# Reordering the probability transposes, one set of statistics and the tails of a two-layer graph kernel

## The chip, the cores and the metric

The kernel runs on one core of one Trainium2 chip, in one launch. The metric is the device time in microseconds of that core. The kernel before was run three times: 2000.07, 2002.58 and 2004.22 us, median 2002.58. A further execution was taken by the hardware profiler; the trace and every profile line here come from that one.

## The reference

The input x is 128 graphs of 128 nodes with 512 features, `adj` is a 128 by 128 matrix. All arithmetic is in float32.

```python
# layer 0: W1 = W2 = adj, so C - A is the bias alone
A = einsum('od,bdn->bon', adj, x)
out = max(relu(A[:, :, None, :] + b), axis=-1)     # one number per graph and row
x = layernorm(x + out)
# layer 1: attention with 8 heads of 64, masked by adj == 0
q, k, v = split(x @ w_qkv)
attn = softmax(where(adj == 0, -inf, q @ k.T / 8))
o = (attn @ v) @ w_proj + b_proj
o = o + layernorm(o) * ln_gamma + ln_beta
x = layernorm(x + o)
```

So each graph goes through one layer norm after layer 0 ("y"), one on the projected attention ("o") and one on the final sum ("z").

## The kernel before, in words

A tile is one graph, 128 nodes on the partitions by 512 features. Four tiles make a group (g, 32 of them), two tiles a pair (q). The three large products (QK, V and the output projection) are done a group at a time by Winograd's form of Strassen's method: a `Unit` has seven half-size products instead of eight. `product(i)` issues the eight matmuls of product i into one of four PSUM banks (b1 to b4; bank 1 takes 1, 6 and 7, bank 2 takes 2, bank 3 takes 5 and 3, bank 4 takes 4). `snap(k)` is a ScalarE copy of bank 1 after products 1, 6 and 7 (k = 1, 2, 3). `result(half, col)` is a VectorE addition of a bank and a snap: (0, 0) reads bank 2 and snap 1, (0, 1) bank 3 and snap 2, (1, 0) bank 4 and snap 3, (1, 1) bank 3 and snap 3. Product 3 adds into bank 3 only after result(1, 1) has read it, and product 6 into bank 1 only after snap 1. Products 5, 6, 7 and 3 need sums of input quarters (`x_sums`, `o_sums`, made mostly on GpSimd by `run_sums`); 1, 2 and 4 take the quarters as they are. The weights have such sums too (`weight_sums`, GpSimd).

The order of the work is written out by hand: `pin` keeps each instruction in program order on its engine, and each engine runs its own list in order. DMAs go through the queue of SP, which is in order too.

The main loop (p = 0 to 60) handles one pair, tiles a = 2p and b = 2p+1, beside one unit of QK for the next group (`first`) and one unit of V or of the output projection (`second`; V where p is odd, but for p = 0, whose first unit is V and whose second is QK). For each tile: `scores` (TensorE), `softmax_max` (VectorE), `softmax_exp` (ScalarE, eight heads), `softmax_div` (VectorE), then the probabilities must be transposed across partitions. `prob_transpose` makes 32 by 32 block transposes into the tile `pu` (VectorE, L421), `prob_write` sends it to a buffer `hop` in DRAM (one DMA, L430), and `prob_read` fetches it back in the other order as `pT` (four DMAs, L441). `prob_move` is the three in a row. `attend` (TensorE, PSUM tile `po`) multiplies pT with V in the next iteration; `attend_copy` takes it out (ScalarE).

Meanwhile later pairs pass through layer 0 (`l0_mm`, `l0_max`, `l0_add`, `l0_norm`, and the same way through DRAM: `l0_transpose`, `l0_write`, `l0_read`, the latter x1T), and earlier ones through their tails: `one` or `stats` takes the mean and variance of tiles (`bn`, two VectorE instructions of 0.66 and 0.18 us each), `finish_stats` makes scale and shift of them (GpSimd, three small instructions), `tail_inner` and `tail_outer` apply them (ScalarE), `tail_residual` does the three additions and multiplications (GpSimd), `tail_store` or `tail_outer_one` writes the output. `tail_fused` does the inner norm and the residual of one tile in three VectorE instructions.

Before the loop, the head runs layer 0 for the first ten tiles and QK of group 0 in two units, with the statistics "first", "second" and "third". After the loop, the tail (from `before, o_u, v_u = ...`) does the last three output projections, of which the last half group (tiles L-3 to L, L = 127) goes through `last_project`, a plain product with the whole weight.

Of the kernel before, what the change touches and what calls it, by code (L numbers as in the profile page):

```python
# [9 lines left out]
F32 = mybir.dt.float32  # L10
# [6 lines left out]
def kernel(  # L17
# [31 lines left out]
    B, P, D = x.shape  # L49
# [3 lines left out]
    G = 4  # L53
    GT = G * P
    HT = GT // 2
    HE = D // 2
# [58 lines left out]
    def weight_sums(w, cols, width):  # L115
        t = w[:, :, :, ds(cols, width)]
        b11, b21, b22, b12 = (t[:, i] for i in range(4))
        tt(nc.gpsimd, t[:, 4], b12, b11, ALU.subtract)
        tt(nc.gpsimd, t[:, 6], b22, b12, ALU.subtract)
        tt(nc.gpsimd, t[:, 5], b22, t[:, 4], ALU.subtract)  # L120
        tt(nc.gpsimd, t[:, 3], b21, t[:, 5], ALU.subtract)
# [273 lines left out]
    def softmax_exp(b, heads=range(H)):  # L395
        if 0 in heads:
            psums[b] = small.tile([P, H], F32, tag="sums", name=f"sums_{b}")
        for i in heads:
            pin(
                nc.scalar.activation(  # L400
                    prob[b][:, i],
                    prob[b][:, i],
                    AF.Exp,
                    bias=nmax[b][:, i : i + 1],
                    accum_out=psums[b][:, i : i + 1],
                )
            )
# [195 lines left out]
    def stats(name, *items):  # L603

        mv = small.tile([P, NC, 2], F32, tag="mv", name=f"mv_{name}")
        for k, (kind, b) in enumerate(items):
            bn({"o": o_of, "z": zs.get, "y": xs.get}[kind](b), mv, k)
        finish_stats(mv, items)
        return mv
# [32 lines left out]
    for q in range(2):  # L642
        l0_beta(q)
        l0_spill(q)
    cur.result(0, 0)
    cur.product(6)
    cur.snap(2)
    cur.product(5)
# [2 lines left out]
    for f in range(G, 2 * G):  # L651
        l0_max(f)
        l0_add(f)
    cur.product(4)
    cur.product(7)
    stats("second", *(("y", f) for f in range(G, 2 * G)))
    before = cur


# [2 lines left out]
    weight_load(wp, w_proj, 0, HE, 0, HE)  # L662
    ga_bc = broadcast(nc.sync, "ga_bc", ln_gamma)
    bp_bc = broadcast(nc.sync, "bp_bc", b_proj)
    weight_sums(wv, 0, HE)
    before.snap(3)
    before.result(1, 1)
    before.result(1, 0)
    for f in range(G, G + 2):
        l0_norm(f)  # L670
    cur.product(2)
# [34 lines left out]
    for p in range(LAST + 1):  # L706
# [66 lines left out]
        if p == 0:  # L773
            first.snap(2)
            scores(a)
            scores(b, ("po", "pa"))
            softmax_max(a)
            softmax_max(b)
            softmax_exp(a)
            softmax_exp(b)  # L780
        else:
            softmax_exp(b, range(4))
            first.snap(2)
            softmax_exp(b, range(4, H))
        first.product(5)
        first.product(4)
        first.product(7)
        if n is not None:
            l0_read(n)
        softmax_div(a)  # L790
        prob_move(a)
        if ph == 1 and tb is not None:
            one("z", zs, tb)
        if ph == 0 and ta is not None:
            one("o", o_rows, ta)
        first.snap(3)
        softmax_div(b)
        prob_move(b)
        first.result(1, 1)
        first.result(1, 0)  # L800
        if f is not None:
            for j in range(2):
                l0_mm(2 * f + j, f"pss{j}")
# [134 lines left out]
    prob_read(L - 3)  # L938
    scores(L - 1)
    v_u.result(1, 1)  # L940
    for t in range(L - 11, L - 7):
        tail_inner_one(t)
    tail_residual_one(L - 11)
    softmax_max(L - 1)
    scores(L, po_pa)
    v_u.result(1, 0)
    run_sums(o_sums(NG - 2))
    o_u = o_unit(NG - 2)
    o_u.product(1)
    o_u.snap(1)  # L950
# [5 lines left out]
    o_u.result(0, 0)  # L956
    v_u.product(3)
    v_u.result(0, 1)
    for t in range(L - 10, L - 7):
        tail_residual_one(t)  # L960
    o_u.product(6)
    softmax_exp(L, range(4))
# [4 lines left out]
    o_u.product(7)  # L967
    softmax_div(L - 1)
    prob_move(L - 1)
    attend(L - 3)  # L970
    o_u.snap(3)
    attend_copy(L - 3)
# [1 line left out]
    attend_copy(L - 2)  # L974
    tail_outer(B // 2 - 7)
    tail_store(B // 2 - 7)
    o_u.result(1, 1)
    softmax_div(L)
    prob_move(L)
    o_u.result(1, 0)  # L980
    o_u.product(3)
    o_u.result(0, 1)
    stats("last_2", ("o", L - 5), ("o", L - 4), ("z", L - 11), ("z", L - 10))
    last_project(L - 3, wlast, "b2")
    last_project(L - 2, wlast, "pss0")
    for t in (L - 5, L - 4):
        tail_inner_one(t)
        tail_residual_one(t)
    attend(L - 1)
    attend_copy(L - 1)  # L990
    for t in (L - 11, L - 10):
        tail_outer_one(t)
    last_project(L - 1, wlast, "pss1")
    stats("last_3", ("z", L - 9), ("z", L - 8), ("o", L - 7), ("o", L - 6))
    mv = stats("last_4", ("o", L - 3), ("o", L - 2))
    for t in (L - 7, L - 6):
        tail_inner_one(t)
        tail_residual_one(t)
    attend(L, "pa")
    attend_copy(L)  # L1000
    last_project(L, wlast, "b1")
    for t in (L - 9, L - 8):
        tail_outer_one(t)
    tail_fused(L - 3, mv[:, 0, 0:1])
    tail_fused(L - 2, mv[:, 1, 0:1])
    mv = stats("last_5", ("o", L - 1), ("z", L - 5), ("z", L - 4))
    mv2 = stats("last_6", ("o", L), ("z", L - 3), ("z", L - 2))
    tail_fused(L - 1, mv[:, 0, 0:1])
    for t in (L - 5, L - 4):
        tail_outer_one(t)  # L1010
    tail_fused(L, mv2[:, 0, 0:1])
    for t in (L - 3, L - 2):
        tail_outer_one(t)
    stats("last_7", ("z", L - 1), ("z", L - 7), ("z", L - 6))
    stats("last_8", ("z", L))
    for t in (L - 1, L - 7, L - 6, L):
        tail_outer_one(t)


# [39 lines left out]
```

## Time and profile before

| what | value |
|---|---|
| median of three runs | 2002.58 us |
| profiled execution, its own time | 2008.6 us |
| its span, first to last instruction | 2006.8 us |
| mean granted TensorE clock | 0.993 |
| busy: TensorE matmul, VectorE, ScalarE, GpSimd | 1956.4, 1607.1, 1055.5, 1266.7 us |
| TensorE busy from 0 to 50, 50 to 100 us | 37.94, 48.59 us |
| TensorE busy from 100 to 1900 us, in the trace's six stretches | 98.62, 396.71, 397.92, 396.99, 397.87, 98.24 us |
| TensorE busy from 1970 to 2007 us | 15.27 us |
| last matmul begins | 1988.07 us |
| issue to landing, median: hop write, pT read, x1T read | 3.7, 3.0, 3.4 us |

The page gives for each engine its busy time, its share of the span and its instructions. PE is TensorE's matmuls, PEld its weight loads, DVE VectorE, ACT ScalarE, POOL GpSimd, SP the engine that issues most DMAs. A line of a timeline reads: start in us, duration in us, engine, source line, operation, output and input by the program's names, shapes, count, and in brackets how long the engine stood idle before it and what ended that. A line of the waits reads: who waited for whom, total us, times, longest. Many operations pass through helpers, so L74 is every matmul and L77 every two-operand addition of VectorE and GpSimd; the names of the tiles tell them apart. A DMA instruction's duration is only its issue.

### The profile page before, as it was taken

To read this page: it belongs to the slowest core of one execution; us is meant where nothing else is said; L and a number is where in the kernel's file an instruction comes from. 1 tells how busy PE (TensorE), PEld (TensorE's weight loads), DVE (VectorE), ACT (ScalarE), POOL (GpSimd) and SP (SyncE) were. 2 spreads that over 40 slices of the span, in tenths; PEclk is the share of its full clock that TensorE was granted. 3 is DMA by queue.
4 is the path that set the end of the run, shared out by engine and by line. 5 is a ranking of instruction groups with operands and counts; after the bars stand their busy time and mean duration, and the time that the engine had idled before them with its cause. 6 is when DMAs were issued, how large, how long until landed. Compare 5 with 4: busy or idle time off the path is not lost.

```text
span 2006.8 us, 33038 instructions
## 1 busy us (share of the span) xinstructions
PE 1956.4 (97%) x11545; PEld 1637.6 (82%) x11545; DVE 1607.1 (80%) x2519; ACT 1055.5 (53%) x3066; POOL 1266.7 (63%) x811
## 2 busy tenths in 40 slices
PE   7999999999999999999999999999999999999995
PEld 5888888888888888888888888888888888888872
DVE  6768778778788788788787888788787887787686
ACT  3444555545545546556555555555455455455453
POOL 5336656767557676557676567576566675576646
PEclk8999999999999999999999999999999999999998
DMA  6655565565565566666556656655665655655553
GB/s 199 153 149 147 162 194 156 172 188 149 178 186 161 179 171 175 179 167 179 179 160 175 191 158 176 191 158 168 184 164 172 188 164 172 186 165 163 157 183 111
DMA packets 445655, 341.76 MB, mean 170 GB/s; under 512 B 276912, under 2 KB 378416, under 8 KB 445488
## 3 DMA queue, kind: packets, MB, share of 16 engines
q1 hardware_dynamic: 445056, 338.85, 58.7%
q8 instruction: 92, 1.51, 0.3%
q10 hardware_dynamic: 432, 0.79, 0.1%
q14 instruction: 75, 0.61, 0.1%
HBM read 172.82 MB, written 166.72 MB: 169 GB/s over the span
## 4 chain that ended last, share of the span: by engine, by line
PE 72%; DVE 13%; DMA 10%; SPq 2%; issue 2%; POOL 1%; ACT 1%; ACTq 0%; POOLq 0%; DVEq 0%
PE b_qk L74 30%; PE b_v L74 14%; PE b_o L74 13%; PE pss L74 6%; PE po L74 5%; DMA hop<-pu 5%; DVE s L77 4%; PE pa L74 3%; DMA pT<-hop 3%; DVE pu L421 2%; SPq L441 1%; DVE xt L287 1%; DVE qk L179 1%; DVE st_mv L235 1%; DVE amax L267 1%
## 5 line engine op out<-in xcount | busy, mean ns | idle before, releaser
L74 PE MATMUL b_qk<-s_x,wqk 128*128 128x256 f32 x2048 | 476.2, 381 | 4.9 <-DVE s_x L77 2.5
L74 PEld LDWEIGHTS b_qk<-s_x,wqk 128*128 128x128 f32 x2048 | 385.9, 190 | 67.6 <-DVE qk L179 11.4
L400 ACT ACTIVATE s<-s,nmax 128x128 f32<-128x128 f32 x1024 | 396.1, 391 | 7.7 <-DVE nmax L393 7.7
L74 PE MATMUL b_qk<-x1T,wqk 128*128 128x256 f32 x1536 | 361.0, 385 | 2.2 <-ACT u_v L173 1.4
L74 PEld LDWEIGHTS b_qk<-x1T,wqk 128*128 128x128 f32 x1536 | 287.9, 191 | 48.5 <-ACT u_v L173 2.2
L77 DVE TENSOR_TENSOR s<-s,rec 128x1024 f32<-128x1024 f32 x128 | 297.0, 2320 | 4.4
L246 POOL TENSOR_SCALAR rs_mv<-mv 128x6 f32<-128x6 f32 (+2 forms) x61 | 14.8, 242 | 418.1 <-DVE mv L236 418.1
L77 POOL TENSOR_TENSOR z<-z,ga_bc 128x1024 f32<-128x1024 f32 x58 | 164.8, 2841 | 177.7 <-ACT z L254 177.7
L173 ACT COPY u_qk<-b_qk 128x512 f32<-128x512 f32 x192 | 112.5, 586 | 250.8 <-PE b_qk L74 249.6
L74 PE MATMUL b_v<-wv,s_x 128*128 128x256 f32 x1024 | 237.0, 379 | 0.0
L74 PE MATMUL b_o<-wp,s_o 128*128 128x256 f32 x992 | 230.0, 380 | 1.8 <-POOL s_o L77 1.8
L381 DVE SCALAR_TENSOR_TENSOR s<-pss,mask 128x512 f32<-128x512 f32 x256 | 164.4, 684 | 70.1 <-PE pss L74 69.7
L74 PEld LDWEIGHTS b_v<-wv,s_x 128*128 128x128 f32 x1024 | 194.4, 190 | 26.8 <-DVE s L77 0.3
L74 PEld LDWEIGHTS b_o<-wp,s_o 128*128 128x128 f32 x992 | 188.1, 190 | 28.5 <-POOL s_o L77 2.2
L77 POOL TENSOR_TENSOR x<-x,be_bc 128x1024 f32<-128x1024 f32 x64 | 182.1, 2847 | 35.4 <-DVE rec L411 28.8
L179 DVE TENSOR_TENSOR v<-b_v,u_v 128x512 f32<-128x512 f32 x128 | 87.1, 681 | 138.2 <-PE po L74 133.0
L400 ACT ACTIVATION_READ_ACCUMULATOR s<-s,nmax 128x1 f32 x1024 | 194.2, 190 | 0.0
L179 DVE TENSOR_TENSOR qk<-b_qk,u_qk 128x512 f32<-128x512 f32 x256 | 167.6, 674 | 31.6 <-PE b_qk L74 16.1
L74 PE MATMUL b_v<-wv,x1T 128*128 128x256 f32 x768 | 176.2, 379 | 0.0
L173 ACT COPY u_v<-b_v 128x512 f32<-128x512 f32 x96 | 56.2, 586 | 226.4 <-PE b_v L74 226.4
L74 PEld LDWEIGHTS b_v<-wv,x1T 128*128 128x128 f32 x768 | 145.9, 190 | 32.2 <-issue 13.9
L173 ACT COPY u_o<-b_o 128x512 f32<-128x512 f32 x93 | 54.5, 586 | 222.9 <-PE b_o L74 222.8
(107 smaller groups left out, 3377.4 us busy)
## 6 DMA issues: line engine op xcount, KB each, us to landing
hop<-pu SPq DMA_DIRECT2D x128, 512.0 KB, 3.7
pT<-hop SPq DMA_DIRECT2D x512, 128.0 KB, 3.0
spill<-x SPq DMA_DIRECT2D x64, 512.0 KB, 4.3
x<-in_x_dram SPq DMA_DIRECT2D x62, 512.0 KB, 4.5
xhop<-xt SPq DMA_DIRECT2D x248, 128.0 KB, 2.3
x1T<-xhop SPq DMA_DIRECT2D x248, 128.0 KB, 3.4
xr<-spill SPq DMA_DIRECT2D x59, 512.0 KB, 3.6
out_dram<-xr SPq DMA_DIRECT2D x58, 512.0 KB, 3.6
```

The lines of the kernel that those rows point to most:

```text
L74: pin(nc.tensor.matmul(*args, **kwargs))
L77: pin(eng.tensor_tensor(dst, a, b, op))
L173: pin(nc.scalar.copy(t, self.banks[1]))
L179: nc.vector.tensor_tensor(self.out[half, col], self.banks[bank], self.snaps[k], ALU.add)
L235: pin(nc.vector.bn_stats(st, src))
L246: pin(nc.gpsimd.tensor_scalar(rs[:, :n], mv[:, :n, 1], EPS, None, ALU.add))
L267: pin(nc.vector.tensor_reduce(amax, pas.pop(f), AX.X, ALU.max))
L287: nc.vector.transpose(xts[q][:, :, :, j].rearrange("p q c b -> p c q b"), xs[2 * q + j].rearrange("p (c q a) -> p c q a", c=KC, q=Q),)
L381: nc.vector.scalar_tensor_tensor(s[:, par], pss[b][par], SCALE, mask.unsqueeze(1).to_broadcast([P, NP, P]), ALU.mult, ALU.add,)
L400: nc.scalar.activation(prob[b][:, i], prob[b][:, i], AF.Exp, bias=nmax[b][:, i : i + 1], accum_out=psums[b][:, i : i + 1],)
L421: nc.vector.transpose(u.rearrange("p q h b -> p h q b"), prob.pop(b).rearrange("p h (q a) -> p h q a", q=Q),)
L441: nc.sync.dma_start(out=pT[b][ds(q * QS, QS)].rearrange("a i h b -> a i (h b)"), in_=hop[:, :, q].rearrange("i a f -> a i f"),)
```

## The change

The change moves instructions; it adds and removes only small ones (two groups of tail statistics are merged with others).

- Head: product(4) of the first unit goes ahead of product(6); the four-tile statistics "second" go behind result(1, 1) and result(1, 0) of that unit, which stand in the next block, and ahead of the weight sums of `wv`.
- Loop: `prob_move` is taken apart. On SP the order is now: write of a, the x1T reads (`l0_read`), write of b, reads of a, reads of b. The statistics `one(...)` between the two tiles go behind the two results. For p = 0, snap(3) goes ahead of the exponentials of b.
- Tail: the sums `o_sums(NG - 2)` go ahead of the four inner norms, the residual of L-11 goes to the other three, `prob_move(L)` goes ahead of attend(L-3), attend(L) and its copy go straight behind attend(L-1), and statistics, residuals and outer norms of the last twelve tiles are dealt out anew.

```diff
     cur.result(0, 0)
+    cur.product(4)
     cur.product(6)
     cur.snap(2)
     cur.product(5)
...
-    cur.product(4)
     cur.product(7)
-    stats("second", *(("y", f) for f in range(G, 2 * G)))
     before = cur
...
-    weight_sums(wv, 0, HE)
     before.snap(3)
     before.result(1, 1)
     before.result(1, 0)
+    stats("second", *(("y", f) for f in range(G, 2 * G)))
+    weight_sums(wv, 0, HE)
...
             softmax_exp(a)
-            softmax_exp(b)
         else:
...
         first.product(7)
+        if p == 0:
+            first.snap(3)
+            softmax_exp(b)
+        softmax_div(a)
+        prob_transpose(a)
+        prob_write(a)
         if n is not None:
             l0_read(n)
-        softmax_div(a)
-        prob_move(a)
+        if p > 0:
+            first.snap(3)
+        softmax_div(b)
+        prob_transpose(b)
+        prob_write(b)
+        prob_read(a)
+        prob_read(b)
+        first.result(1, 1)
+        first.result(1, 0)
         if ph == 1 and tb is not None:
             one("z", zs, tb)
         if ph == 0 and ta is not None:
             one("o", o_rows, ta)
-        first.snap(3)
-        softmax_div(b)
-        prob_move(b)
-        first.result(1, 1)
-        first.result(1, 0)
...
     v_u.result(1, 1)
+    run_sums(o_sums(NG - 2))
     for t in range(L - 11, L - 7):
         tail_inner_one(t)
-    tail_residual_one(L - 11)
     softmax_max(L - 1)
     scores(L, po_pa)
     v_u.result(1, 0)
-    run_sums(o_sums(NG - 2))
...
-    for t in range(L - 10, L - 7):
+    for t in range(L - 11, L - 7):
         tail_residual_one(t)
...
     prob_move(L - 1)
+    softmax_div(L)
+    prob_move(L)
     attend(L - 3)
...
     tail_store(B // 2 - 7)
+    mv = small.tile([P, NC, 2], F32, tag="mv", name="mv_last_2")
+    keys = [("z", L - 11), ("z", L - 10), ("o", L - 5), ("o", L - 4), ("o", L - 7), ("o", L - 6)]
+    bn(zs[L - 11], mv, 0)
+    bn(zs[L - 10], mv, 1)
     o_u.result(1, 1)
-    softmax_div(L)
-    prob_move(L)
     o_u.result(1, 0)
+    bn(o_of(L - 5), mv, 2)
+    bn(o_of(L - 4), mv, 3)
     o_u.product(3)
     o_u.result(0, 1)
-    stats("last_2", ("o", L - 5), ("o", L - 4), ("z", L - 11), ("z", L - 10))
     last_project(L - 3, wlast, "b2")
     last_project(L - 2, wlast, "pss0")
-    for t in (L - 5, L - 4):
-        tail_inner_one(t)
-        tail_residual_one(t)
     attend(L - 1)
     attend_copy(L - 1)
+    attend(L, "pa")
+    attend_copy(L)
+    last_project(L - 1, wlast, "pss1")
+    last_project(L, wlast, "b1")
+    bn(o_of(L - 7), mv, 4)
+    bn(o_of(L - 6), mv, 5)
+    finish_stats(mv, keys)
+    for t in (L - 5, L - 4, L - 7, L - 6):
+        tail_inner_one(t)
     for t in (L - 11, L - 10):
         tail_outer_one(t)
-    last_project(L - 1, wlast, "pss1")
-    stats("last_3", ("z", L - 9), ("z", L - 8), ("o", L - 7), ("o", L - 6))
-    mv = stats("last_4", ("o", L - 3), ("o", L - 2))
-    for t in (L - 7, L - 6):
-        tail_inner_one(t)
-        tail_residual_one(t)
-    attend(L, "pa")
-    attend_copy(L)
-    last_project(L, wlast, "b1")
+    tail_residual_one(L - 5)
+    mv = stats("last_3", ("o", L - 3), ("o", L - 2), ("z", L - 9), ("z", L - 8))
+    tail_residual_one(L - 4)
     for t in (L - 9, L - 8):
         tail_outer_one(t)
     tail_fused(L - 3, mv[:, 0, 0:1])
     tail_fused(L - 2, mv[:, 1, 0:1])
-    mv = stats("last_5", ("o", L - 1), ("z", L - 5), ("z", L - 4))
-    mv2 = stats("last_6", ("o", L), ("z", L - 3), ("z", L - 2))
+    mv = stats("last_4", ("o", L - 1), ("z", L - 3), ("z", L - 2))
+    tail_residual_one(L - 7)
     tail_fused(L - 1, mv[:, 0, 0:1])
+    for t in (L - 3, L - 2):
+        tail_outer_one(t)
+    mv = stats("last_5", ("o", L), ("z", L - 5), ("z", L - 4))
+    tail_residual_one(L - 6)
+    tail_fused(L, mv[:, 0, 0:1])
     for t in (L - 5, L - 4):
         tail_outer_one(t)
-    tail_fused(L, mv2[:, 0, 0:1])
-    for t in (L - 3, L - 2):
-        tail_outer_one(t)
-    stats("last_7", ("z", L - 1), ("z", L - 7), ("z", L - 6))
-    stats("last_8", ("z", L))
-    for t in (L - 1, L - 7, L - 6, L):
+    stats("last_6", ("z", L - 1), ("z", L - 7))
+    stats("last_7", ("z", L), ("z", L - 6))
+    for t in (L - 1, L - 7, L, L - 6):
         tail_outer_one(t)
```

## Prediction

> **What bounds the kernel now.** First the engine line and the clock line of the page: TensorE is busy 97% of the span at full clock, so time can come only from the few stretches in which it stands still, or from the ends.
>
> ```profile
> PE 1956.4 (97%) x11545; PEld 1637.6 (82%) x11545; DVE 1607.1 (80%) x2519; ACT 1055.5 (53%) x3066; POOL 1266.7 (63%) x811
> PEclk8999999999999999999999999999999999999998
> ```
>
> Second, the waits of TensorE over the span (total us, times, longest).
>
> ```profile
> PE po L74 <- DMA pT<-hop: 11.5, 19, 1.2
> ...
> PE b_qk L74 <- DVE s_x L77: 2.5, 1, 2.5
> ...
> PE b_qk L74 <- ACT u_v L173: 1.4, 1, 1.4
> ...
> PE b_qk L74 <- ACT u_qk L173: 0.7, 1, 0.7
> ```
>
> In the main loop only the transposed probabilities pT come late, and by little. The waits of the weight loads add one that the matmul rows hide:
>
> ```profile
> PEld b_qk L74 <- DVE qk L179: 11.4, 28, 2.1
> ```
>
> These are 28 times that product(3) of the first unit waits for VectorE to read bank 3 (result(1,1)). Third, TensorE's timeline at the `po` groups. Its late ones look like this, always the second group, tile b:
>
> ```profile
> 1054.54 1.09 PE L74 MATMUL po<-pT,v 128*64 128x128 f32 x16
> 1056.84 1.09 PE L74 MATMUL po<-pT,v 128*64 128x128 f32 x16 [1.21 <-DMA pT<-hop]
> ```
>
> From the start of one iteration's first po group to the next I get 60 periods. The shortest are 29.97 us for even p and 30.18 us for odd p; what all 60 have above these sums to 16.0 us, the full price of late pT. Fourth, the queue of SP in one iteration:
>
> ```profile
> 1007.66 2.75 SPq L318 DMA_DIRECT2D x1T<-xhop  x4
> 1010.46 0.82 SPq L430 DMA_DIRECT2D hop<-pu  x1
> 1014.38 1.73 SPq L441 DMA_DIRECT2D pT<-hop  x4
> 1016.21 0.38 SPq L430 DMA_DIRECT2D hop<-pu  x1
> 1019.81 1.73 SPq L441 DMA_DIRECT2D pT<-hop  x4
> ```
>
> The write of b stands behind the reads of a, which stand until the write of a has landed. Fifth, the chain of waits in the head, which ends in TensorE's 0.7 us wait:
>
> ```profile
> 39.89 0.19 DVE mv_second L236
> ...
> 40.16 0.23 POOL rs_mv_second L246
> ...
> 41.84 1.52 ACT x L254 x2
> 43.35 0.48 ACT u_qk L173
> ...
> 43.97 3.69 PE b_qk L74 x16
> ```
>
> Last, the tail: VectorE restarts at 1981.91 and sets the end; TensorE waits for a copy that ScalarE does late.
>
> ```profile
> 1981.91 0.75 DVE L595 SCALAR_TENSOR_TENSOR z<-z,rs_mv_last,pp 128x512 f32<-128x512 f32 x1 [5.86 <-POOL rs_mv_last L77]
> ...
> 1982.96 5.18 PE L74 MATMUL pp<-wlast,oT 128*128 128x512 f32 x8 [3.17 <-ACT oT L471]
> ```
>
> [...] a hop write lands a median 3.7 us after its issue, and SP issues nothing in between. [...] the division `s<-s,rec` takes 1.22 us beside an idle POOL and 2.0 to 2.75 us beside a busy one. [...] the clock records change on a grid of 3.413 us; after the window at 1979.15, with 0.63 us of matmuls, the clock is 0.5 for 3.41 us; after windows with 1.36 us it drops and with 1.68 us it does not.
>
> **The change, part by part.** All sums are against the profiled execution (2008.6 us, span 2006.8); its 6.0 us above the median of 2002.58 stay out, and I subtract the sum from the median.
>
> *Loop, pT.* Taking the iteration shown: the two statistics of 0.8 us between the tiles go behind the results, so pu of b is ready 1.6 us sooner (1015.1 to 1013.5). The write of a goes at about 1009.6 (its pu ends at 1009.5), the four x1T reads behind it at 1010 to 1012.8, the write of b at 1013.5 instead of 1016.2, the reads of a at 1013.9 (hop landed at 1013.3), those of b at 1013.5 + 3.7 = 1017.2 instead of 1019.8. That is 2.6 us sooner; in even p the same count gives 3.8. The worst period lost 1.4 us, so the margin covers nearly all; I leave 1.0 us for stray slow landings: **-15.0** (bounds -16.0 and -8). Moved with it: x1T reads 2.3 us later (used some ten us later by the next group's sums; hidden), and out, spill, reload and load issues some 2 us sooner (they wait for nothing that moves). Reads of a start within 0.5 us of before.
>
> *Loop, product(3).* Statistics now follow result(1,1), which ends near 1014.1 instead of 1015.65; product(3) is due at 1015.6. The stall is two steps of about 0.105 us (108 and 104 ns above the usual matmul spacing) in 28 odd iterations: 28 x 0.21 = **-5.9** (bounds -5.9 and 0). l0_max keeps its place, since VectorE's total ahead of it is unchanged.
>
> *Head.* product(4) needs no sums, so its 1.73 us fill the 2.5 us wait before product(6). But this frees TensorE only to wait elsewhere. The statistics "second" leave VectorE at 36.77 and now stand behind result(1,1) and (1,0), which wait for snap(3), which follows the last l0_add on ScalarE (37.65) and takes 0.6: results 38.25 to 39.5, statistics 39.5 to 43.0 instead of 36.77 to 40.27. Queued behind them: POOL's rs and sh (1.65), two norms (1.5), snap(1) (0.5); product(6) of the second unit, which needs bank 1 read, starts at 46.7 instead of 43.97: **+2.75** (bounds +1.5, +3.2). TensorE is out of work from 41.8, so one window lies nearly empty and the next runs at half clock: 3.41/2 = **+1.7** (0 to +3.4). All that follows is TensorE-bound to 68.8, so nothing gives this back. Weight sums of wv slip from 46.8 to 49.5 on POOL; used at 57.8 + 4, hidden.
>
> *p = 0.* snap(3) no longer follows the exp of b: the 1.41 us wait at 70.22 goes. But exp(b) then runs 67.65 to 70.75 instead of 66.5 to 69.6, division and transpose of b end 1.1 us later, and result(1,1) behind them at 74.1 instead of 73.05; product(3), due at 72.2, starts at 74.2 instead of 73.78: **+0.4** (bounds -1.4, +2.1 with a clock drop).
>
> *Tail.* Sums s_o ahead of the residual of L-11: the 1.75 us wait at 1949.57 goes, but product(5) still waits for v_u.result(0,1) (VectorE, to 1950.94): -0.3. Division and pu of L fill VectorE's idle 1954.4 to 1960; write of L goes behind the reads of L-1 at 1962, its pT lands near 1970, before it is used at 1972.9; the output of pair 57 stands behind these on SP, 4 us later, and nobody waits for it. attend(L) follows attend(L-1), so TensorE ends near 1983.3 instead of 1989.2, but that end was not last. The tail_inner of L-5 now stands behind attend_copy(L) on ScalarE (1974.6), one residual (3.95) and rs (1.4) follow on POOL: VectorE restarts at 1980.85 instead of 1981.91. From there: two fused tails 5.0, three statistics 2.4, rs 1.3, rest of a fused tail 1.7, statistics 2.4, rs 1.3, 1.7; POOL's last residual (4.4) ends at about 1999, two rs chains (2.5) and two norms (1.5) follow: last output issued near 2003.4 instead of 2003.75. **-0.4** (bounds -1.5, +1.5). The new statistics waits are the price: VectorE did 18.5 us without one.
>
> **Sum:** -15.0 - 5.9 + 2.75 + 1.7 + 0.4 - 0.4 = -16.45; 2002.58 - 16.45 = **1986.1** (profiled execution: about 1992).
>
> **Rivals.**
> *Half of the loop's gain.* Three hop writes and reads overlap more, landings grow past 3.7 us and b's margin shrinks: pT gives -8, or the product(3) step stays (it may be the cost of a changed operand, not of a wait; against that, even p do not have it). Time: 1986.1 + 6 or 7 = 1992.5.
> *Head hidden.* If the norms wait less than I count, or no clock drop comes (-2.9), and p = 0 and the tail fall at their good ends (-1.8 and -1.1), the time is 1980. For it: the page shows only 3.2 us of waits in the head. Against: the chain of norms is plain.
> *Slower: SP blocked by b.* Reads of a now stand behind the write of b. They land at about 1018.7 and are used at 1024.6: 5.9 us of margin. If b's pu slips by more than that (division behind a slow POOL), every further 0.1 us costs 60 x 0.1 = 6 us, and the -15 is lost too. At 0.3 us past the point: 2002.6 + 18 + 4.5 = 2025. Against: the dearest division seen costs 1.5 us extra.
> *Nothing.* Loop gives only product(3) (-5.9) and head takes 4.9: 2001.5.
>
> **Chances.** Forecast 0.58 (1983 to 1990), half gain 0.18, head hidden 0.15, nothing 0.05, slower 0.04. The range leaves out the last two and the edges: 1979 to 1996. A change under 0.2% (4 us) can't be told from none here. Faster 0.92, same 0.04, slower 0.04.
>
> **What would show it.** The row of po waits on pT falls from 11.5 us to under 1.5; periods are 29.97 for both parities; SP shows two hop writes before eight pT reads; a wait of about 5 us for u_qk near 46.7 and a half clock after it; a wait of product(3) for qk or v near 77 (shifted). A po wait in the first group would make me wrong, as would a product(6) that starts before 45.

## The result and the profile after

| kernel | runs | median, us | lowest to highest, us |
|---|---|---|---|
| before | 4 | 2002.80 | 2000.07 to 2004.22 |
| changed | 4 | 1987.91 | 1985.16 to 1988.53 |

The ratio is 0.9925 [0.9907, 0.9942]: 14.9 us less (11.6 to 18.6 by the interval). That is some 1.8 us above the 1986.1 predicted and well inside its range. The profiled execution of the changed kernel took 1988.53 us, its span 1986.7 us. It is one of the four runs, while the profiled execution of before (2008.6 us) lay 6 us above the median of its kernel.

The page first, its engine line, its clock line and the shares of the chain that ended last, by engine:

```profile
PE 1946.4 (98%) x11545; PEld 1644.8 (83%) x11545; DVE 1565.2 (79%) x2518; ACT 1055.1 (53%) x3066; POOL 1293.7 (65%) x808
PEclk8999999999999999999999999999999999999997
...
PE 95%; DVE 2%; DMA 1%; POOL 1%; ACT 0%; issue 0%; SPq 0%; ACTq 0%; POOLq 0%; DVEq 0%
```

In before the same line read:

```profile
PE 72%; DVE 13%; DMA 10%; SPq 2%; issue 2%; POOL 1%; ACT 1%; ACTq 0%; POOLq 0%; DVEq 0%
```

Now it is TensorE nearly from end to end: the chain no longer leaves it in the loop for the way of the probabilities through DRAM. The waits of TensorE say what is left (who waited for whom, total us, times, longest):

```profile
PE b_qk L74 <- ACT u_qk L173: 3.9, 1, 3.9
...
PE b_v L74 <- DVE v L179: 2.0, 1, 2.0
...
PE po L74 <- DMA pT<-hop: 1.0, 1, 1.0
```

The waits on pT fell from 11.5 us in 19 to 1.0 us in one, and that one is in the tail. The rows for s_x (2.5 us) and for u_v (1.4 us) are gone; the row for u_qk grew from 0.7 to 3.9 us (in the head), and that for v (2.0 us, at p = 0) is new; the prediction named both. In the weight loads' waits the row of 28 waits on qk, 11.4 us in all, is no longer there.

The queue of SP in one iteration (issue start, issue duration):

```profile
1001.48 0.34 SPq L430 DMA_DIRECT2D hop<-pu  x1
1001.86 3.20 SPq L318 DMA_DIRECT2D x1T<-xhop  x4
1005.11 1.11 SPq L430 DMA_DIRECT2D hop<-pu  x1
1006.31 4.76 SPq L441 DMA_DIRECT2D pT<-hop  x8
```

The write of a goes first, the four x1T reads behind it, then the write of b, and only then the eight reads of pT.

The span can be cut in three by the starts of TensorE's po groups: up to that of p = 1 (the head and p = 0), from there to that of p = 61, and the rest.

| stretch, us | before, as shown | before, profiled again | changed |
|---|---|---|---|
| start to the first po group | 82.51 | 81.74 | 87.25 |
| p = 1 to p = 61 | 1820.33 | 1813.92 | 1794.76 |
| p = 61 to the end | 103.95 | 103.92 | 104.74 |
| span | 2006.8 | 1999.6 | 1986.7 |

In the changed kernel 58 of the 60 periods are 29.97 us and the last two, which have no matmuls of layer 0, 28.25 us: 58 x 29.97 + 2 x 28.25 = 1794.8. The loop is TensorE's own work and nothing else. It gained 19.2 to 25.6 us, and the head and p = 0 gave 4.7 to 5.5 us of it back.

### The profile page after: what moved, and what is told of

Same layout as the page of the kernel before. It is cut to its first block, busy times and chain, and to the rows that moved or that the text cites. A ratio compares the mean times of both kernels' runs of the same rounds, so it can differ in the third digit from the quotient of the medians.

```text
span 1986.7 us, 33036 instructions
## 1 busy us (share of the span) xinstructions
PE 1946.4 (98%) x11545; PEld 1644.8 (83%) x11545; DVE 1565.2 (79%) x2518; ACT 1055.1 (53%) x3066; POOL 1293.7 (65%) x808
## 4 chain that ended last, share of the span: by engine, by line
PE 95%; DVE 2%; DMA 1%; POOL 1%; ACT 0%; issue 0%; SPq 0%; ACTq 0%; POOLq 0%; DVEq 0%
PE b_qk L74 39%; PE b_v L74 19%; PE b_o L74 19%; PE pss L74 6%; PE po L74 6%; PE pa L74 5%; PE pp L74 0%; POOL zl L77 0%; DMA x<-in_x_dram 0%; DMA wqk<-in_L_gnn_w_qkv_dram 0%; DVE s_x L77 0%; DMA hop<-pu 0%; DVE st_mv_last L235 0%; DVE z L77 0%; POOL rs_mv_last L77 0%
## 5 line engine op out<-in xcount | busy, mean ns | idle before, releaser
L74 PEld LDWEIGHTS b_qk<-s_x,wqk 128*128 128x128 f32 x2048 | 391.8, 191 | 58.1 <-POOL wv L77 4.3
L77 DVE TENSOR_TENSOR s<-s,rec 128x1024 f32<-128x1024 f32 x128 | 252.3, 1971 | 4.4
```

Source lines behind the costliest of these rows:

```text
L74: pin(nc.tensor.matmul(*args, **kwargs))
L77: pin(eng.tensor_tensor(dst, a, b, op))
```

## The experiments

My theory: in the loop two separate causes go, the late pT of tile b and the stall of product(3) behind the statistics; in the head the delayed norms and a clock drop give some 5 us back; p = 0 and the tail are worth under 1 us. The rivals are those of the prediction: a loop gain of half the size, a head that costs nothing, and SP's new order as a danger. Medians of the kernels are compared with one another directly, though the batches of experiments ran on three different chips. The median of before itself was 2002.80 us beside the changed kernel and 2004.37, 2001.14 and 1999.38 us in the batches. Its late pT differ from execution to execution, as shown below; what part the chip has in this was not separated. The kernels without late pT repeat within 0.6 to 4.0 us, and `old_p0` and `old_tail`, which should lie within 0.6 us of the changed kernel, came within 0.7 us of it in another batch.

### The loop alone, and its two halves

`loop_only` is before with the change of the loop and nothing else: the head, the tail and the two exponentials and snap(3) of p = 0 are as before. Against before:

```diff
+        softmax_div(a)
+        prob_transpose(a)
+        prob_write(a)
         if n is not None:
             l0_read(n)
-        softmax_div(a)
-        prob_move(a)
-        if ph == 1 and tb is not None:
-            one("z", zs, tb)
-        if ph == 0 and ta is not None:
-            one("o", o_rows, ta)
         first.snap(3)
         softmax_div(b)
-        prob_move(b)
+        prob_transpose(b)
+        prob_write(b)
+        prob_read(a)
+        prob_read(b)
         first.result(1, 1)
         first.result(1, 0)
+        if ph == 1 and tb is not None:
+            one("z", zs, tb)
+        if ph == 0 and ta is not None:
+            one("o", o_rows, ta)
```

> The kernel before with the loop's part of the change alone (head, first iteration and tail as before). My theory: the loop gives all of the gain and head, first iteration and tail cost some 5 us of it (in the profiled executions the first po group starts 4.7 us later and the stretch from the last iteration to the end is 0.7 us longer), so this is FASTER than the full change: about 1982.5 us, every period 29.97 us. Rival, the later start of the full change is only the jitter of the first loads: then this is equal to the full change, about 1988 us.

Measured: 1982.86 us, ratio 0.9893 [0.9878, 0.9908], against 2004.37 us for before in this batch: 21.5 us less. The prediction's two terms of the loop are 20.9. Its waits of TensorE hold no row of po on pT at all, and all its periods are 29.97 (28.25 for the last two).

`stats_only` moves only the statistics; each tile's write and reads stay together. Against before:

```diff
-        if ph == 1 and tb is not None:
-            one("z", zs, tb)
-        if ph == 0 and ta is not None:
-            one("o", o_rows, ta)
         first.snap(3)
         softmax_div(b)
         prob_move(b)
         first.result(1, 1)
         first.result(1, 0)
+        if ph == 1 and tb is not None:
+            one("z", zs, tb)
+        if ph == 0 and ta is not None:
+            one("o", o_rows, ta)
```

> The kernel before with one edit: the two statistics between the tiles go behind the two results; the queue of SP keeps its order. My theory: only the wait of product(3) goes (28 x 0.21 us and the 1.7 us wait in the one iteration without layer 0), since the write of b still stands behind the reads of a: -7.5 us, about 1995 us; the waits of po on pT stay near 10 us. Rival, b is late because VectorE finishes it late: then the earlier pu takes the pT waits away as well, about 1984 us.

`queue_only` is `loop_only` with the statistics left between the tiles. Against `loop_only`:

```diff
         prob_write(a)
         if n is not None:
             l0_read(n)
+        if ph == 1 and tb is not None:
+            one("z", zs, tb)
+        if ph == 0 and ta is not None:
+            one("o", o_rows, ta)
         first.snap(3)
...
         first.result(1, 1)
         first.result(1, 0)
-        if ph == 1 and tb is not None:
-            one("z", zs, tb)
-        if ph == 0 and ta is not None:
-            one("o", o_rows, ta)
```

> The kernel before with the other edit alone: write of a, x1T reads, write of b, reads of a, reads of b, with the statistics left between the tiles. My theory: the reads of b issue 1.0 us (odd p) to 2.3 us (even p) sooner, so the pT waits fall from 11.5 us to below 2 and the product(3) stalls of 0.21 us in odd iterations stay: -12 us, about 1991 us. Rival, the two DMAs side by side land later and eat the lead: pT waits of 6 us or more, about 1997 us.

Measured: `stats_only` 1991.67 us, 0.9937 [0.9924, 0.9949], 12.7 us less than before; `queue_only` 1990.24 us, 0.9928 [0.9914, 0.9942], 14.1 us less. The waits of TensorE in `stats_only`:

```profile
PE po L74 <- DMA pT<-hop: 4.9, 9, 1.0
```

And those in `queue_only`, of matmuls and of weight loads:

```profile
PE b_qk L74 <- DVE qk L179: 1.7, 1, 1.7
```

```profile
PEld b_qk L74 <- DVE qk L179: 11.6, 28, 2.1
```

Each half takes away what it should. With the statistics moved, product(3) no longer waits, and part of the late pT remains. With SP reordered, no pT is late, and the 28 stalls stay: the periods of `queue_only` alternate between 29.97 and 30.17 to 30.20 us. From its first po group to that of p = 61 it takes 1802.64 us, 7.9 more than `loop_only` (1794.76), and by the medians the statistics are worth 7.4 us on top of the reordered queue. So product(3) is a term of 7.9 us, not of 5.9: the prediction missed p = 59, whose period is 30.19 us in `queue_only` and 28.25 in `loop_only`. The row of 1.7 us above is that iteration, where product(3) has no matmuls of layer 0 to hide behind.

I had put `stats_only` at 7.5 us, which was too little. Tile b stands so close to its due time that moving the statistics takes away part of the waits as well: its loop takes 1803.68 us, 8.9 above `loop_only`. The late pT of before cost 17.7 and 11.3 us in its two profiles (25.6 and 19.2, less 7.9 for product(3)), so between a fifth and a half of them went. The halves add up to 26.8 us where both together give 21.5: what one of them does for pT, the other need not do again.

`before_again` is the kernel before, unchanged.

> The kernel before, profiled a second time. My theory: its waits on pT change from execution to execution, since tile b lands within 1 us of its use; the first profiled execution (2008.6 us, 11.5 us of waits) was a slow one, and one near the median of 2002 shows 5 to 8 us of waits and the same 28 product(3) stalls. Rival, the waits are the same and the 6 us lay elsewhere.

It took 2001.37 us (one execution, span 1999.6), and its waits of TensorE have this row:

```profile
PE po L74 <- DMA pT<-hop: 6.6, 14, 1.0
```

The first profile had 11.5 us in 19. The late pT are thus worth 17.7 us in the first profile and 11.3 in the second: the same kernel differs by 6 us in this one term. The end of the kernel does not differ (103.95 and 103.92).

What the new order does to the DMAs shows in the times ahead of the po group that uses them, medians over the loop for even p / odd p (tile b's are used about 1 us after the group's start):

| us ahead of the po group | before | changed |
|---|---|---|
| write of a issued | 13.56 / 13.95 | 15.42 / 14.83 |
| pT of a landed | 4.94 / 5.36 | 4.86 / 4.12 |
| write of b issued | 7.97 / 8.06 | 11.75 / 11.18 |
| write of b landed | 3.81 / 4.30 | 7.56 / 6.82 |
| pT of b landed | -0.95 / -0.31 | 2.44 / 1.93 |

In even p tile b landed 0.95 us after the group's start, which is just when it is used; now it has 3.4 us to spare. It comes 3.4 and 2.2 us sooner, where I had counted 3.8 and 2.6: the write of b now takes 4.2 us to land (3.7 before), and its four reads 4.8 us from the first issue to the last landing (4.4 before).

### SP held up

`reads_last` puts all pT reads behind the rest of SP's work of the iteration: out, spill, the reload of xr and the load. It stands for the slower rival. This diff, and all that follow, are against the changed kernel.

```diff
         prob_write(b)
-        prob_read(a)
-        prob_read(b)
...
         if p + 6 < B // 2:
             load(p + 6)
+        prob_read(a)
+        prob_read(b)
```

> The full change with all eight pT reads moved to the end of SP's iteration, behind the output, the spill, the reload and the load, two of which wait for a landing. It tests the slower rival of the prediction, that reads held back on SP cost every iteration. My theory: the reads of a begin some 5.5 us later and land about when they are used, those of b land 1 us late: about 60 us in all, 2048 us (2020 to 2100). Rival, there is slack enough: 1990 us.

Measured: 2356.33 us (one execution, span 2354.5), 368 us above the changed kernel, where I had expected some 60. SP's queue, the waits of TensorE, one of the late groups, and the page's engine and clock lines:

```profile
417.84 0.68 SPq L430 DMA_DIRECT2D hop<-pu  x1
418.56 0.43 SPq L560 DMA_DIRECT2D out_dram<-xr  x1
423.07 0.33 SPq L331 DMA_DIRECT2D spill<-x  x1
423.50 0.38 SPq L530 DMA_DIRECT2D xr<-spill  x1
425.93 0.38 SPq L100 DMA_DIRECT2D x<-in_x_dram  x1
426.40 5.04 SPq L441 DMA_DIRECT2D pT<-hop  x8
```

```profile
PE po L74 <- DMA pT<-hop: 230.6, 95, 5.9
```

```profile
433.61 1.97 PE L74 MATMUL po<-pT,v 128*64 128x128 f32 x16 [3.79 <-DMA pT<-hop]
```

```profile
PE 2084.2 (89%) x11545; PEld 1750.8 (74%) x11545; DVE 1546.6 (66%) x2518; ACT 1055.0 (45%) x3066; POOL 1291.6 (55%) x808
...
PEclk8999899998989989989899998989999999999998
```

The spill waits at the head of the queue (418.99 to 423.07), the load waits another 2.0 us, and the reads are issued 8.6 us after the write of b instead of 1.2. A pT read then lands a median 5.7 us after its issue, by the page, where the changed kernel has 3.7. The 3.79 us wait of TensorE also cost clock: from 433.6 to 440 us it was granted 0.54, and the 16 matmuls above took 1.97 us, where in the changed kernel 32 of them take 1.97. In most of the loop the periods are 35 to 38 us.

So the cliff that the rival named is real, and the page says what it is made of. The waits on pT grew by 229.6 us (1.0 to 230.6), and TensorE's busy time by 137.8 us (1946.4 to 2084.2) for the same 11545 matmuls: together 367.4 of the 367.8 us between the two spans. Here each us of waiting cost 0.6 us of slower matmuls on top. The rival's price, 0.1 us per iteration for each 0.1 us of lateness, left that out. My 60 us counted 5.5 us of delay for the reads, where this iteration shows 7.4, and no clock.

### The head

`old_head` is the changed kernel with the head of before.

```diff
     cur.result(0, 0)
-    cur.product(4)
     cur.product(6)
...
+    cur.product(4)
     cur.product(7)
+    stats("second", *(("y", f) for f in range(G, 2 * G)))
     before = cur
...
+    weight_sums(wv, 0, HE)
     before.snap(3)
     before.result(1, 1)
     before.result(1, 0)
-    stats("second", *(("y", f) for f in range(G, 2 * G)))
-    weight_sums(wv, 0, HE)
```

> The full change with the head of before (product(4) behind the layer 0 matmuls, statistics ahead of the results). My theory: the 3.9 us wait and the half clock behind it go, the short waits of before come back: -4.3 us against the full change, about 1983.6 us, and the first po group starts near 83 us. Rival, the head's later start is jitter: no change, 1988 us.

Measured: 1982.64 us, 0.9890 [0.9877, 0.9904]: 5.3 us below the changed kernel. The head's edit is a loss, of the size that the prediction gave it (4.45). Its chain of waits in the changed kernel:

```profile
41.22 0.19 DVE mv_second L236
...
41.49 0.23 POOL rs_mv_second L246
...
43.87 0.80 ACT x L254
44.66 0.48 ACT u_qk L173
...
45.28 6.54 PE b_qk L74 x16
```

And TensorE's timeline there (the view runs from 40 to 50 us and cuts both rows):

```profile
39.67 1.68 PE L74 MATMUL b_qk<-s_x,wqk 128*128 128x256 f32 x7
45.28 5.03 PE L74 MATMUL b_qk<-s_x,wqk 128*128 128x256 f32 x11 [3.93 <-ACT u_qk L173]
```

The same links as before (statistics, rs, norms, snap(1)), only later: TensorE runs out of work at 41.35 and waits 3.93 us. Then 16 matmuls, which took 3.69 us in before, take 6.54: the granted clock is 0.5 from 44.21 us for 6.83 us.

`hold_clock` fills that gap with four matmuls into a bank that nobody reads, behind the product(3) that comes last before the wait. They are extra work; everything else is the changed kernel.

```diff
     cur.result(0, 0)
     before.product(3)
+    idle = psum.tile([P, D], F32, tag="pss0", name="idle")
+    for _ in range(4):
+        pe(idle, lhsT=adjT, rhs=be_bc, start=True, stop=True)
     before.result(0, 1)
```

> The full change with four more matmuls, which nobody reads, in the head's wait for snap(1) (3.4 us of work in a gap of 5.5). My theory: the half clock behind that gap is a cost of its own, 2.9 us in the profiled execution (the 16 matmuls at 45.28 took 6.5 us instead of 3.7); with the gap filled the clock stays whole and the kernel gets FASTER by doing more: about 1985 us, no clock of 0.5 near 44 us. Rival, the clock is not what slows those matmuls: no change or slightly slower, 1988 us.

Measured: 1984.50 us, 0.9919 [0.9905, 0.9932]: 3.4 us below the changed kernel, and 2.7 and 3.1 below `old_p0` and `old_tail`, which ran beside it on the same chip. TensorE's timeline (the four matmuls are eight records):

```profile
41.56 3.60 PE L74 MATMUL idle<-be_bc,adjT 128*128 128x512 f32 x8
45.65 3.69 PE L74 MATMUL b_qk<-s_x,wqk 128*128 128x256 f32 x16 [0.49 <-ACT u_qk L173]
```

Product(6) does not start sooner (45.65 against 45.28), but its 16 matmuls are back at 3.69 us and the granted clock is 1.0 from 44.2 to 51.1 us, where the changed kernel has 0.51. The difference is the clock drop and nothing else, since the wait for the norms is untouched. A kernel that does more is faster by about what the drop costs: 2.85 us in the changed kernel's profile (6.54 - 3.69).

`snap_before_norms` keeps product(4) ahead of product(6), puts the statistics back ahead of the results, and lets ScalarE make snap(1) before the norms, on which it doesn't depend.

```diff
     cur.product(7)
+    stats("second", *(("y", f) for f in range(G, 2 * G)))
     before = cur
...
-    stats("second", *(("y", f) for f in range(G, 2 * G)))
     weight_sums(wv, 0, HE)
-    for f in range(G, G + 2):
-        l0_norm(f)
     cur.product(2)
     cur.product(1)
     cur.snap(1)
+    for f in range(G, G + 2):
+        l0_norm(f)
```

> The full change with the head mended: product(4) stays first, the statistics go back ahead of the results, and snap(1) of the second unit goes ahead of the two norms that wait for the statistics. My theory: the chain statistics, norms, snap(1), product(6) is what costs the head; off that chain TensorE has no wait from 27 us to the first iteration, so this beats even the full change with the old head (1982.6) by the 2.4 us of waits left there: about 1980.5 us. Rival, the transposed tiles of the next group then come too late, for their norms are half a us later: a new wait near 67 us, and 1983 us or more.

Measured: 1980.79 us, 0.9899 [0.9884, 0.9914], 7.1 us below the changed kernel. TensorE's timeline has no bracket left there:

```profile
36.33 3.62 PE L74 MATMUL b_qk<-x1T,wqk 128*128 128x256 f32 x16
39.98 5.45 PE L74 MATMUL b_qk<-s_x,wqk 128*128 128x256 f32 x24
45.27 1.88 PE L74 MATMUL pa<-x,adjT 128*128 128x512 f32 x4
```

It is also 1.9 us below `old_head`. So with the statistics back and snap(1) out of the norms' way, product(4) ahead of product(6) does no harm and seems to pay: its 1.7 us lie in the wait for s_x. No run has product(4) alone, nor the statistics back without snap(1) moved, so the shares of the three are not separated.

The traces show a second use of product(4), which neither the prediction nor these experiments looked for. Of the six profiles that have before's order in this place, two show a slow product(6) of the first unit right behind the wait for s_x: in `loop_only` and `queue_only` it takes 5.38 us instead of 3.69. The 1.7 us more are what `old_p0` lost behind its wait for the norms (5.38 against 3.69 as well), at a mean granted clock of 0.75; that a half clock is the cause here too is an estimate from that.

```profile
27.97 5.38 PE L74 MATMUL b_qk<-s_x,wqk 128*128 128x256 f32 x16 [2.59 <-DVE s_x L77]
```

With product(4) first that wait is at most 0.49 us, and product(6) takes 3.69 us in the changed kernel, `hold_clock`, `snap_before_norms` and `best`.

### p = 0 and the tail

`old_p0` is the changed kernel with p = 0 in the order of before:

```diff
             softmax_exp(a)
+            softmax_exp(b)
...
-        if p == 0:
-            first.snap(3)
-            softmax_exp(b)
...
-        if p > 0:
-            first.snap(3)
+        first.snap(3)
```

> The full change with the first iteration's exponentials in the old order (both tiles ahead of snap(3)). My theory: product(3)'s wait of 2.0 us on result(1,1) goes and the 1.4 us wait on snap(3) comes back: -0.4 us, so 1987.5 us, told only by the trace. Rival, the new order is worth the 1.4 us that it takes away: 1989.3 us.

`old_tail` is the changed kernel with the whole tail of before; of its diff only the core:

```diff
     prob_move(L - 1)
-    softmax_div(L)
-    prob_move(L)
     attend(L - 3)
...
     o_u.result(1, 1)
+    softmax_div(L)
+    prob_move(L)
     o_u.result(1, 0)
...
     attend(L - 1)
     attend_copy(L - 1)
-    attend(L, "pa")
-    attend_copy(L)
...
+        tail_residual_one(t)
+    attend(L, "pa")
+    attend_copy(L)
     last_project(L, wlast, "b1")
```

> The full change with the tail of before. My theory: from the last iteration's po group to the end the new tail takes 0.7 us more, so this is 1987.2 us; TensorE ends some 6 us later and it does not matter. Rival, TensorE's earlier end counts: then this is slower, about 1992 us.

Measured: `old_p0` 1987.24 us, 0.9931 [0.9919, 0.9944]; `old_tail` 1987.63 us, 0.9934 [0.9921, 0.9946]. Neither can be told from the changed kernel by its time. In the profiles: the changed kernel, and then `old_p0`, at product(3) and product(1) of p = 0:

```profile
78.41 2.00 PE L74 MATMUL b_v<-wv,s_x 128*128 128x256 f32 x8 [1.99 <-DVE v L179]
```

```profile
73.29 3.72 PE L74 MATMUL b_qk<-x1T,wqk 128*128 128x256 f32 x16 [1.41 <-ACT u_v L173]
```

The 1.41 us wait for snap(3) has gone, and one of 1.99 us for result(1, 1) has come: +0.6 us in TensorE's waits, predicted +0.4. The tail, from the po group of p = 61 to the end, takes 103.93 us in `old_tail` and 103.47 to 103.48 in four kernels with the new one (`hold_clock`, `old_p0`, `old_head`, `snap_before_norms`): -0.45 us, predicted -0.4. The changed kernel's own profile shows 104.74, since there one pT came late after the loop (1939.19, 1.03 us).

The old tail is not always 103.9 us long, though. Four of its six profiles show that; `loop_only` and `stats_only` show 105.07 and 105.00. There one of the last products took 6.6 and 6.5 us instead of 5.2 to 5.4, behind the same wait of 3.2 us, and VectorE had to wait for it. In the first profile of before the granted clock was 0.5 from 1982.56 to 1985.97 us under this product (5.18 us); that it lasted longer in these two is an estimate from the product's time. In `loop_only`:

```profile
1958.58 6.62 PE L74 MATMUL pp<-wlast,oT 128*128 128x512 f32 x8 [3.16 <-ACT oT L471]
...
1966.29 0.70 DVE L235 BATCH_NORM_STATS2 st_mv_last<-pp 128x6 f32<-128x512 f32 x1 [1.04 <-PE pp L74]
```

Against those two the new tail is 1.5 to 1.6 us shorter.

`inner_early` asks why so much moved work is worth so little. It moves the last two statistics, the four inner norms and two outer norms ahead of attend(L-1) and its copy.

```diff
+    bn(o_of(L - 7), mv, 4)
+    bn(o_of(L - 6), mv, 5)
+    finish_stats(mv, keys)
+    for t in (L - 5, L - 4, L - 7, L - 6):
+        tail_inner_one(t)
+    for t in (L - 11, L - 10):
+        tail_outer_one(t)
     attend(L - 1)
     attend_copy(L - 1)
     attend(L, "pa")
     attend_copy(L)
     last_project(L - 1, wlast, "pss1")
     last_project(L, wlast, "b1")
-    bn(o_of(L - 7), mv, 4)
-    bn(o_of(L - 6), mv, 5)
-    finish_stats(mv, keys)
-    for t in (L - 5, L - 4, L - 7, L - 6):
-        tail_inner_one(t)
-    for t in (L - 11, L - 10):
-        tail_outer_one(t)
     tail_residual_one(L - 5)
```

> The full change with one more edit in the tail: the statistics of L-7 and L-6, the four inner norms and the two outer ones go ahead of the last two attends, so that ScalarE does them while it would wait for attend(L-1). My theory: those norms stood ready for 7 us behind a copy that waited for TensorE; with them early the residual of L-5 is done before the statistics it shares GpSimd with, VectorE restarts 4.6 us sooner and the end follows: about 1983.3 us. Rival, the chain behind (statistics, rs, fused tails in turn) has slack of its own: 1986 us or more.

Measured: 1984.54 us, 0.9920 [0.9907, 0.9932], 3.4 us below the changed kernel by the medians; in the profile the stretch from p = 61 to the end is 98.89 us instead of 103.5, which is 4.6. In the changed kernel, ScalarE and then VectorE:

```profile
1952.52 0.58 ACT L471 COPY oT<-po 128x512 f32<-128x512 f32 x1 [10.20 <-PE po L74]
...
1953.80 2.93 ACT L254 ACTIVATE zl<-o,sh_mv_last,rs_mv_last 128x512 f32<-128x512 f32 x4
```

```profile
1959.99 0.75 DVE L595 SCALAR_TENSOR_TENSOR z<-z,rs_mv_last,pp 128x512 f32<-128x512 f32 x1 [5.21 <-POOL rs_mv_last L77]
```

In `inner_early`:

```profile
1945.31 2.93 ACT L254 ACTIVATE zl<-o,sh_mv_last,rs_mv_last 128x512 f32<-128x512 f32 x4 [4.82 <-POOL sh_mv_last L77]
...
1950.66 0.59 ACT L471 COPY oT<-po 128x512 f32<-128x512 f32 x1 [1.01 <-PE po L74]
```

```profile
1953.55 0.75 DVE L595 SCALAR_TENSOR_TENSOR z<-z,rs_mv_last,pp 128x512 f32<-128x512 f32 x1 [0.61 <-POOL rs_mv_last L77]
```

ScalarE stood 10.2 us behind a copy that waited for TensorE, with four inner norms in its queue behind it; GpSimd's residual and its scale for VectorE came behind those. Taken out of that queue, VectorE's wait falls from 5.21 to 0.61 us. TensorE's end counts little: it starts its last matmuls at 1961.52 in the changed kernel and 1967.65 in `old_tail`, 6.1 us later, for 0.45 us of time. Only in the two profiles with the slower product was it waited for.

### All that helped, together

`best` is the changed kernel with the head of `snap_before_norms`, the tail of `inner_early`, and for p = 0 the two results ahead of the division of b.

```diff
         if p > 0:
             first.snap(3)
+        else:
+            first.result(1, 1)
+            first.result(1, 0)
         softmax_div(b)
...
         prob_read(b)
-        first.result(1, 1)
-        first.result(1, 0)
+        if p > 0:
+            first.result(1, 1)
+            first.result(1, 0)
```

> The loop's change, the mended head (product(4) first, statistics ahead of the results, snap(1) ahead of the norms), in the first iteration snap(3) ahead of b's exponentials and the two results ahead of b's division, and the tail with the inner norms early. My theory, from the mended head's 1980.8: the 2.0 us wait of product(3) in the first iteration goes, and 4.6 us of the tail: about 1974.2 us. Rival, the gains share a wait: 1977 us.

Measured: 1974.60 us (1974.06 to 1976.28), 0.9875 [0.9860, 0.9890]: 13.3 us below the changed kernel, and below every other kernel here. The 1.99 us wait of product(3) at p = 0 has gone. The only wait of TensorE that is left between 55 and 95 us is this one, of a later product:

```profile
PE b_qk L74 <- DVE v L179: 0.2, 1, 0.2
```

## Why the prediction was right, step by step

- **What bounds it.** Right. TensorE's periods fell to its own work, 29.97 us for both parities, and both rows of late waits went from the loop.
- **Loop, pT (-15.0).** The mechanism is shown by `queue_only` and `loop_only`; tile b comes 3.4 and 2.2 us sooner (predicted 3.8 and 2.6). The size is not one number: 17.7 us in the first profile of before, 11.3 in the second, and 21.5 - 7.9 = 13.6 by the medians of its batch (8.6 to 12.0 against the other medians of before). The prediction's 16.0 us was too low by 1.7 for its own profile, for the most part since it judged p = 60, whose period without layer 0 is 28.25 us, by 29.97. And it took the term from an execution 6 us above the median and set it against the median without taking that surplus out of it.
- **Loop, product(3) (-5.9).** The mechanism is shown by `queue_only`; that it might be the cost of a changed operand falls with it, since only the statistics differ from `loop_only`. The term was mis-sized: it is 7.9 us, 27 stalls of 0.22 us and 1.9 us at p = 59, which the prediction counted as one more 0.21. This error and the one above have opposite signs against the medians. That their sum, -20.9, met -21.5 is luck. Against the profile that it was worked from, the sum promised about 1992 us, and the changed kernel's profile took 1988.53.
- **Head chain (+2.75).** Right in kind and near in size. In the profile of before the last statistics end at 40.08 us and in the changed kernel at 41.40; product(6) starts at 43.97 and 45.28. Both are 1.3 us, but VectorE ran late in that profile of before. Product(6) starts at 42.42 to 43.97 us in the four profiles that have the head of before and a first product(6) of 3.69 us, and at 44.78 to 45.84 in the six with the changed head: 2.3 us later by the means.
- **Half clock (+1.7).** That the clock is lost to the hole is shown by `hold_clock`; the size is not one number. Behind a wait of 3.9 us the same 16 matmuls took 6.54 us in the changed kernel (the clock 0.5 for 6.83 us; 2.85 us more than the 3.69 of before) and 6.36 in `old_tail` (0.51 from 44.2 to 51.1 us), but 5.38 in `old_p0` (0.75 in that stretch; 1.7 us more) and in `inner_early`. In the changed kernel TensorE was busy for 0.55 us of the 3.41 us up to 44.21, and for 2.34 of the next 3.41, at 0.5. What decides between the two sizes was not shown.
- **p = 0 (+0.4) and tail (-0.4).** +0.6 and -0.45 by the profiles, the tail -1.5 to -1.6 where the old one had the slower product; by the times neither can be told from nothing. The reason that the tail gives so little is shown by `inner_early`: the inner norms' place behind attend_copy, which the prediction named.
- **The 1.8 us.** Head, clock and p = 0 come to some 5.7 us in the changed kernel's profile, where the prediction has 4.85. By the medians everything outside the loop costs 1987.91 - 1982.86 = 5.05 us, against 4.45. Both explain part of the 1.8 us, but the interval of the result is wider than that, so it can't be shared out.
- **Half of the loop's gain.** Fell: `loop_only` has no late pT and no stall. **Nothing** fell with it.
- **Head hidden.** Fell: `old_head` is 5.3 us below the changed kernel.
- **Slower.** SP's order did no harm here, with 4.1 to 4.9 us of margin for tile a (5.9 predicted). That the margin exists is why the change is safe. The rival's 2025 us also left out the 5.9 us of product(3), which its sum keeps; with them it is 2019. `reads_last` shows the far side, at a much larger overrun than the 0.3 us priced there.

Left open: how much of the head's loss each execution pays. The first po group of kernels with the head of before starts anywhere from 80.89 to 83.71 us. The two latest of the six, 83.34 and 83.71, are those with the first product(6) of 5.38 us; without them the range is still 80.89 to 82.51.

## What to carry to other kernels

When TensorE is busy 97% of a span, measure the periods of its loop and compare them with the shortest one: stalls of a few tenths, which a wait row shows in part or only for the weight loads, add up there to their full price (7.9 us for product(3)). When a step is moved behind others on an in-order engine, list what is queued behind it (here norms and a snap that do not depend on one another), and put first what TensorE waits for; and do not count work out of a stall without asking whether the hole that is left can cost clock (behind the 3.93 us one here it was 0.5 for 6.83 us). Take the terms of a sum and its base from the same execution, or profile the kernel twice, before a marginal wait is priced.

## What the runs showed of the hardware

- **A hole in TensorE's work cost clock behind it.** After the 3.93 us wait in the changed kernel the granted clock was 0.5 for 6.83 us (2.85 us lost), after that of `old_p0` a mean 0.75 from 44.2 to 51.1 us (1.7 us lost), and after the 3.79 us wait of `reads_last` 0.54 from 433.6 to 440 us. With 3.60 us of idle matmuls and a 0.49 us wait in `hold_clock` it stayed at 1.0.
- **The length of the wait alone did not decide.** Two waits of 3.93 us, in the changed kernel and in `old_p0`, left the same 16 matmuls at 6.54 and 5.38 us. In the head of before, product(6) took 5.38 us behind waits for s_x of 2.6 us (`loop_only`, `queue_only`), and 3.69 behind 2.5 us (the first profile of before, at a clock of 1.0 from 26.72 to 33.55 us, and `stats_only`), 1.84 (`before_again`) and 1.69 us (`old_head`). What else counts was not shown.
- **DMAs that followed others closely landed later.** In the changed kernel a hop write took 3.15 us from issue to landing where it went first (a) and 4.2 right behind the x1T reads (b); in before it took 3.7 to 3.9. The four pT reads of b took 4.4 us from first issue to last landing in before and 4.8 behind the four of a. A single pT read took a median 3.0 us in before, 3.7 in the changed kernel and 5.7 in `reads_last`, where the reads go behind spill, reload and load too. What in the queue or the memory takes that time was not separated. That SP's queue stands still while its next DMA waits is shown by the prediction's own lines, where SP issues nothing from 1011.28 to 1014.38 us.
- **The waits of the weight loads cost less than their row says.** 28 waits are 11.6 us in `queue_only`; the one of 2.1 us aside, 0.35 us each. The periods grew by 0.22 us each, and all of it cost 7.9 us. The row is a sign of a stall, the period is its price.
- **A busy GpSimd did not always slow the division.** The prediction has it at 1.22 us beside an idle GpSimd and at 2.0 to 2.75 beside a busy one. In the profile of before three divisions (66.89, 93.90 and 154.88 us) took 1.22 to 1.23 us although GpSimd began an operation 0.02 to 0.29 us after them, and others with a part of GpSimd's work beside them took 1.5 to 1.9.
